# Scores of a pair's second row one set of products later in an attention-and-experts kernel on Trainium2

## The chip, the cores and the metric

The kernel runs on one core of a Trainium2 chip. The core's engines run side by side, each through its own list of instructions, and wait for each other by semaphores: TensorE (PE in the rows; PEld is its weight load), VectorE (DVE), ScalarE (ACT), GpSimd (POOL), and SyncE (SP), which here only issues DMAs. The metric is the device time of one execution in microseconds; less is better.

## The reference

Eight batch rows of 512 tokens with 256 channels are normalized, attend to 64 context tokens of their row, and go through three experts (768 to 512 to 256 channels), weighted by a softmax router, and through a gate. All is float32.

```
nx = layer_norm(x) ; q = nx @ Wq ; k = ctx @ Wk ; v = ctx @ Wv
weights  = softmax(q k^T * H**-0.5) ; evidence = weights @ v
combined = [nx, evidence, anchor]
probs  = softmax(combined @ router_W + router_b)
h      = silu(combined @ e_w1 + e_b1)           # three experts
routed = sum_e probs_e * (h_e @ e_w2 + e_b2)
g      = sigmoid(silu(combined @ gate_w1 + gate_b1) @ gate_w2 + gate_b2)
out    = x + g * (routed @ out_w + out_b)
```

## The kernel before

Two batch rows make a pair, and the loop at line 1113 runs over four pairs, j = 0 to 3. Row 2j is the pair's first row and 2j + 1 its second; in the stage of pair j, b0 and b1 are the two rows of pair j + 1, which are prepared beside it. Tokens lie along the free dimension (512), channels along the 128 partitions. A product is one matmul of a 128x128 weight with a 128x512 operand. Products of a 2x2 block form (two channel blocks by the two rows) are computed by Strassen's scheme (its Winograd form): seven products in place of eight, with sums and differences of operands formed by VectorE and GpSimd ahead.

Each pair has a gate layer (gate_layer, line 742), three expert layers (expert_layer, line 788) and the outputs stage (outputs, line 866). The order on every engine is the order of the program text; nothing reorders it. What belongs to the next pair is woven in by hand: put() in the loop hangs a step onto a named point, and run(point) emits the steps of that point in the order in which they were put.

The outputs stage runs sets of twelve products through experts(): first u (line 1006), then z with the weight sums S1 (1011), u with S2 (1016), y (1020), u (1024), z with S4 (1027) and u (1030). "S2 set", "y set" and "u set" in this text are lines 1016, 1020 and 1024. Between them VectorE forms differences of the hidden rows (subtract, line 922, whose operation is line 930), keeps partial results (keep, 944) and finishes a quarter of the output (finish, 956): sum (959), gate (960), block transpose into yb (961), then GpSimd adds x (962), and SyncE stores it in eight DMAs (951). The tag yb has two buffers.

The steps of the next pair that matter here:

- transpose_blocks(b), line 504: two VectorE block transposes (509), then two ScalarE scalings (481) that give nxT, the normalized and transposed x
- scores(b), line 523: sixteen small PE products out of nxT into one PSUM bank (531), VectorE takes the maximum (539), scales it (541, tile nmx) and copies the router's part (543, tile lg); ScalarE takes four exponentials with their sums (546)
- softmax(b), line 552: VectorE's reciprocal (555) and one multiplication of the weights w (556)
- router_logits(b), line 570: two products and two reductions over context tokens (576, 582), then four short operations
- combine_x(j + 1), line 512, on GpSimd: four differences of the two rows' nxT (521); the third overwrites a block of b1's nxT and so has to come after b1's scores
- transpose_w(j + 1), line 558, at the point P7: four PE transposes of the softmax weights of both rows, which ScalarE copies to wT

PSUM banks for small steps come from misc(), which hands out three banks in turn in the order of its calls.

Of the kernel before, what the change touches and what calls it, by code (L numbers as in the profile page):

```python
# [16 lines left out]
def kernel(  # L17
# [50 lines left out]
    nc = tc.nc  # L68
# [797 lines left out]
    def outputs(j, steps):  # L866
        last = j == NP - 1

        def run(point):
            for step in steps.get(point, ()):  # L870
                step()
# [40 lines left out]
        def a(q, i, k):  # L912
            return w2o[:, 2 * q + k, i * P : (i + 1) * P]
# [5 lines left out]
        def combo(s):  # L919
            return lambda q: w2s[:, s, q, :]  # L920

        def subtract(dst, other):

            (k, i), (k2, i2), (k3, i3) = dst, *other
            for e in range(E):
                d, p, m = (
                    S["h", ii, e].rearrange("p (q k) t -> p q k t", k=2)[:, :, kk, :]
                    for kk, ii in ((k, i), (k2, i2), (k3, i3))
                )
                nc.vector.tensor_tensor(d, p, m, ALU.subtract)  # L930
# [25 lines left out]
        def finish(r, ps, i, row):  # L956

            yb = work.tile([P, T], F32, tag="yb", name=f"yb_{2 * j + row}_{i}")
            nc.vector.tensor_tensor(r, r, ps, ALU.add)
            nc.vector.tensor_tensor(r, r, S["hg", row, i], ALU.mult)  # L960
            nc.vector.transpose(yb, r)  # L961
            nc.gpsimd.tensor_tensor(yb, yb, S["xb", 2 * j + row][:, i, :], ALU.add)  # L962
            store(yb, i, row, slice(0, T), (nc.sync,))
# [55 lines left out]
        if j + 1 < NP:  # L1019
            experts(y, lambda q: a(q, 0, 1), 1, 0, start=True)  # L1020
            finish(r11, y, 0, 0)
            subtract((0, 1), ((1, 0), (0, 1)))
            run("P2")
            experts(u, lambda q: a(q, 1, 0), 0, 0)
            finish(r22, u, 1, 1)
            run("P7")
            experts(z, combo(S4), 1, 1)
            finish(r12, z, 0, 1)
            run("P3")
            experts(u, lambda q: a(q, 1, 1), 0, 1)  # L1030
            finish(r21, u, 1, 0)
            run("P4")
            return
# [22 lines left out]
    with tc.manual_schedule(engines=None):  # L1056
        ctx_rows = context.flatten_outer_dims().rearrange("(t p) d -> p t d", p=P)
        for d in range(2):
            half = slice(d * NX // 2, (d + 1) * NX // 2)
            nc.sync.dma_start(ctx_sb[:, half, :], ctx_rows[:, half, :])  # L1060
        nc.scalar.dma_start(wk_sb, rows_of(Wk))
        nc.scalar.dma_start(wv_sb, rows_of(Wv))
        load_x(0)
        nc.sync.dma_start(wq_sb, rows_of(Wq))
        load_x(1)
        for g in (E, 0):
            load_first(g)
            load_anchor(g)
        for g in (1, 2):
            load_first(g)  # L1070

        wake(7)
        context_transposes()
        project_keys()
        statistics(0, 0, NT)
        deviation(0, 0)
        normalize(0)
        project(wv_sb, ctxT, lambda m, ps: nc.scalar.copy(vT[:, m, :], ps), "v")
        small_transposes()
        wq_transposes()  # L1080
        transpose_x(0)
        router_anchor()
        statistics(1, 0, NT)
        deviation(0, 1)
        normalize(1)
        load_table(AF.Exp)
        project(wqT, kT, keep_m, "m")
        combine_weights(E)
        value_weights(0, E)
        spread_router_rows(0)  # L1090
        transpose_x(1)
        combine_x(0, nc.vector, (0, 1))
        scores(0)
        scores(1)
        load_table(AF.Silu)
        combine_weights(0)
        softmax(0)
        value_weights(0, 0, nc.vector.tensor_copy)
        anchor_rows(E)
        anchor_rows(0)  # L1100
        softmax(1)
        combine_x(0, nc.vector, (2, 3))
        combine_weights(1)
        combine_weights(2)
        late_scratch()
        load_anchor(1)
        load_anchor(2)
        nc.sync.dma_start(ow_sb, rows_of(out_w))
        nc.sync.dma_start(gw2_sb, rows_of(gate_w2))
        combine_gate()  # L1110
        load_second(0)

        for j in range(NP):


            within, between = {}, {}

            def put(where, n, step, *args):
                where.setdefault(n, []).append(lambda: step(*args))

            if j == 0:
                put(within, "gate", value_weights, 0, 1)
                put(within, (0, "A"), anchor_rows, 1)
                put(within, (0, "A"), router_logits, 0)
                put(within, (0, "A"), load_second, 1)
                put(within, (0, "B"), second_bias)
                put(within, (0, "B"), router_logits, 1)
                put(within, (0, "C"), transpose_second, 0)
                put(within, (0, "C"), anchor_columns, 1)
                put(within, (0, "C"), anchor_rows, 2)  # L1130
                for b in range(2):
                    put(within, (0, "C"), router_exp, b)
                    put(within, (0, "D"), router, b)
                put(within, (0, "C"), load_second, 2)
                put(within, (0, "D"), second_layer, 0)
                put(within, (0, "D"), spread_probabilities, 0)
                put(within, (0, "D"), combine_second, 0)
                put(within, (1, "A"), transpose_second, 1)
                put(within, (1, "B"), second_layer, 1)
                put(within, (1, "B"), combine_second, 1)  # L1140
                put(within, (1, "C"), transpose_second, 2)
                put(within, (1, "C"), anchor_columns, 2)
                put(within, (1, "D"), second_layer, 2)
                put(within, (1, "D"), combine_second, 2)
            if j:
                put(within, "gate end", spread_probabilities, j)
            put(within, (0, "C" if j == 0 else "B"), value_weights, j, 2)
            put(within, (1, "C"), load_x_blocks, 2 * j)
            put(within, (2, "A"), gate_differences, j)
            put(within, (2, "C"), load_x_blocks, 2 * j + 1)  # L1150
            if j + 1 < NP:
                b0, b1 = 2 * j + 2, 2 * j + 3
                put(within, "gate", load_x, b0)
                put(within, "gate", load_x, b1)
                put(within, (0, "A" if j else "D"), statistics, b0, 0, NT)
                put(within, (0, "C") if j else (1, "A"), statistics, b1, 0, NT)
                for i in range(2):
                    put(within, (1, "C"), deviation, j + 1, i)
                where = (1, "D") if j else (2, "B")
                put(within, where, normalize, b0)  # L1160
                put(within, where, store_x, b0)
                put(within, where, regroup_x, b0)
                put(within, (2, "C"), normalize, b1)
                put(within, (2, "C"), store_x, b1)
                put(between, "begin", transpose_blocks, b0)
                put(between, "gate", regroup_x, b1)
                put(between, "P1", scores, b0)
                put(between, "begin", value_weights, j + 1, E)
                put(between, "begin", spread_router_rows, j + 1)
                put(between, "P5", softmax, b0)  # L1170
                put(between, "P5", transpose_blocks, b1)
                put(between, "P6", scores, b1)
                put(between, "P6", router_logits, b0)
                put(between, "P6", softmax, b1)
                put(between, "P6", combine_x, j + 1, nc.gpsimd)
                put(between, "P7", transpose_w, j + 1)
                put(between, "P7", value_weights, j + 1, 0)
                put(between, "P7", router_logits, b1)
                put(between, "P3", value_weights, j + 1, 1)
                put(between, "P3", router_exp, b0)  # L1180
                put(between, "P3", router_exp, b1)
                put(between, "P4", router, b0)
                put(between, "P4", router, b1)
            gate_layer(j, within)
            for e in range(E):
                expert_layer(j, e, within)
            outputs(j, between)
# [34 lines left out]
```

## Time and profile before

| | |
|---|---|
| median of 3 runs | 489.81 us (489.61 to 491.72) |
| profiled execution | 491.32 us, its span 489.6 us |
| mean granted TensorE clock | 0.986 |
| PE busy | 477.2 us, 97% |
| VectorE busy | 350.1 us, 72% |
| ScalarE busy | 218.0 us, 45% |
| GpSimd busy | 77.3 us, 16% |

The span runs from the first to the last instruction of the profiled execution; the rest of its time lies around it. Times in rows are microseconds from the start of the span unless ns stands beside them. A PE row's busy time runs to the modelled end of a pipelined product, so that successive rows overlap a little; in the chain of work that ended last they don't, and there the piece of a set is its share of the time. A granted clock of 1.00 is 2.4 GHz, one of 0.50 is 1.2 GHz. The three stages of pairs 0, 1 and 2 that prepare a next pair end their S2 sets at about 125, 240 and 353 us; the last pair prepares nothing.

### The profile page before, as it was taken

The page shows a single profiled execution, that of the slowest core. Times are in us where ns is not written, and L with a number is a line of the kernel's source. Part 1 is how long each engine was busy: PE and PEld are TensorE (multiplying, and loading weights), DVE is VectorE, ACT ScalarE, POOL GpSimd, SP SyncE. Part 2 cuts the span into 40 slices and gives each one's busy share as a digit, 9 for nine tenths or more (in the row PEclk, how much of TensorE's full clock was granted, in tenths as well). Part 3 has the DMA queues.
Part 4 walks back from the last instruction along what each step waited for, and adds up shares of the span by engine and source line. Part 5 has one row for each costly group of instructions (what it writes and reads, how often), then busy time and mean ns, then how long its engine had stood idle before and what let it go on. Part 6 is the DMA issues. An engine that isn't in the chain of part 4 may idle for free.

```text
span 489.6 us, 4649 instructions
## 1 busy us (share of the span) xinstructions
PE 477.2 (97%) x1451; PEld 227.8 (47%) x1451; DVE 350.1 (72%) x649; ACT 218.0 (45%) x391; POOL 77.3 (16%) x96
## 2 busy tenths in 40 slices
PE   8999999999799999999799999999899999999997
PEld 7744555445444444445444444445354444444454
DVE  2845748989786555889788555898979525787982
ACT  3455565566200556747211365758211254458000
POOL 5326024000412100000232100000042200000010
PEclk9999999999799999999989999999989999999999
DMA  9977230067012550342102550162102380000013
GB/s 283 381 114 151 39 131 0 22 132 63 17 21 43 132 151 0 81 92 43 16 3 42 132 169 2 52 119 44 18 0 43 52 207 0 1 0 1 0 18 68
DMA packets 118120, 35.27 MB, mean 72 GB/s; under 512 B 104732, under 2 KB 115088, under 8 KB 117584
## 3 DMA queue, kind: packets, MB, share of 16 engines
q1 hardware_dynamic: 114736, 27.02, 27.2%
q0 software_dynamic: 1472, 7.18, 4.6%
q10 hardware_dynamic: 1888, 0.79, 0.6%
q8 instruction: 11, 0.18, 0.2%
q14 instruction: 13, 0.11, 0.1%
HBM read 27.57 MB, written 7.40 MB: 71 GB/s over the span
## 4 chain that ended last, share of the span: by engine, by line
PE 89%; DVE 8%; ACT 1%; DMA 1%; issue 1%; DVEq 0%; ACTq 0%
PE ps_u L656 37%; PE ps_z L656 17%; PE ps_y L656 15%; PE ps_vw L631 5%; DVE h L930 4%; PE ps_s L531 3%; PE ps_gu L656 3%; PE ps_w2o L416 2%; PE ps_gz L656 1%; ACT nxT L481 1%; DMA scr_ctx<-in_ctx_dram 1%; DVE h L739 1%; PE ps_k L310 1%; PE ps_v L298 1%; PE ps_gy L656 1%
## 5 line engine op out<-in xcount | busy, mean ns | idle before, releaser
L739 DVE TENSOR_TENSOR h<-h,pb 128x512 f32<-128x512 f32 x96 | 61.9, 694 | 10.5 <-ACT h L689 10.5
L656 PE MATMUL ps_u<-h,w2o 128*128 128x512 f32 x144 | 63.8, 592 | 0.0
L656 PE MATMUL ps_u<-nxT,w 128*128 128x512 f32 x112 | 55.6, 607 | 0.0
L689 ACT ACTIVATE h<-h,abias 128x512 f32<-128x512 f32 x72 | 49.2, 718 | 8.7 <-DVE h L695 8.2
L656 PE MATMUL ps_z<-wT,vw 64*128 64x512 f32 x104 | 49.5, 605 | 0.0
L962 POOL TENSOR_TENSOR yb<-yb,xb 128x512 f32<-128x512 f32 x14 | 21.8, 1555 | 144.6 <-DVE yb L961 130.2
L656 PE MATMUL ps_z<-h,w2s 128*128 128x512 f32 x96 | 42.8, 595 | 0.2 <-DVE r L945 0.2
L656 PEld LDWEIGHTS ps_u<-h,w2o 128*128 128x128 f32 x144 | 27.3, 190 | 32.8 <-issue 30.6
L698 ACT COPY h<-ps_u 128x512 f32<-128x512 f32 x48 | 27.9, 582 | 32.2 <-PE ps_u L656 31.9
L695 DVE TENSOR_TENSOR h<-h,ps_y 128x512 f32<-128x512 f32 x24 | 16.4, 683 | 28.5 <-PE ps_y L656 28.5
L656 PEld LDWEIGHTS ps_u<-nxT,w 128*128 128x128 f32 x112 | 19.9, 189 | 29.7 <-issue 22.8
L930 DVE TENSOR_TENSOR h<-h,h 128x1024 f32<-128x1024 f32 x24 | 31.0, 1345 | 0.0
L689 ACT ACTIVATE h<-ps_u,abias 128x512 f32<-128x512 f32 x24 | 16.5, 687 | 30.4 <-PE ps_z L656 30.4
L656 PE MATMUL ps_y<-nxT,w 128*128 128x512 f32 x56 | 28.6, 592 | 0.0
L656 PE MATMUL ps_z<-T,ws 128*128 128x512 f32 x56 | 28.6, 592 | 0.0
L656 PEld LDWEIGHTS ps_z<-h,w2s 128*128 128x128 f32 x96 | 17.9, 190 | 22.1 <-issue 21.1
L656 PE MATMUL ps_u<-wT,vw 64*128 64x512 f32 x56 | 27.8, 611 | 0.0
L656 PE MATMUL ps_y<-h,w2o 128*128 128x512 f32 (+1 forms) x60 | 27.2, 612 | 0.0
L656 PE MATMUL ps_y<-wT,vw 64*128 64x512 f32 x56 | 27.0, 596 | 0.0
L631 PE MATMUL ps_vw<-w,vT 128*128 128x512 f32 (+1 forms) x64 | 26.9, 541 | 0.0
L656 PE MATMUL ps_u<-T,ws 128*128 128x512 f32 x56 | 26.7, 594 | 0.0
L656 PE MATMUL ps_z<-nxT,ws 128*128 128x512 f32 x56 | 26.6, 592 | 0.0
(206 smaller groups left out, 776.7 us busy)
## 6 DMA issues: line engine op xcount, KB each, us to landing
pb<-pd POOLq DMA_DIRECT2D x4, 1536.0 KB, 7.2
x<-in_x_dram SPq DMA_DIRECT2D x8, 512.0 KB, 5.8
xb<-in_x_dram SPq DMA_DIRECT2D x64, 64.0 KB, 2.5
out_dram<-yb SPq DMA_DIRECT2D x56, 64.0 KB, 2.0
w<-in_L_xcond_e_w_dram SPq DMA_DIRECT2D x6, 512.0 KB, 9.5
xd<-x SPq DMA_DIRECT2D x6, 512.0 KB, 3.0
xg<-xd SPq DMA_DIRECT2D x48, 64.0 KB, 2.4
scr_wa<-in_L_xcond_e_w_dram SPq DMA_DIRECT2D x3, 512.0 KB, 5.0
```

What stands on the lines that cost most here:

```text
L298: nc.tensor.matmul(ps, w_sb[:, k, m * P : (m + 1) * P], src[:, k, :], start=(k == 0), stop=(k == KH - 1))
L310: nc.tensor.matmul(ps[m][:, half], wk_sb[:, k, m * P : (m + 1) * P], ctxT[:, k, half], start=(k == 0), stop=(k == KH - 1),)
L416: nc.tensor.matmul(ps[:, d * H : (d + 1) * H], w2T[:, k, (i + d) * P : (i + d + 1) * P], ow_sb[:, k, :], start=(k == 0), stop=(k == KH - 1),)
L531: nc.tensor.matmul(ps[:, t, :], nxT[:, k, t * P : (t + 1) * P], mr[:, k, b, :], start=(k == 0), stop=(k == KH - 1),)
L631: nc.tensor.matmul(ps, vT[:, k, j * 2 * CT : (j + 1) * 2 * CT], w1[:, KH + k, n0:n1], start=(k == 0), stop=(k == KH - 1),)
L656: nc.tensor.matmul(ps, lhsT, rhs, start=start, stop=True, skip_group_check=not start)
L689: nc.scalar.activation(h, h if src is None else src, AF.Silu, bias=abias[:, c, 2 * j + i : 2 * j + i + 1])
L695: nc.vector.tensor_tensor(h, h, part, ALU.add)
L698: nc.scalar.copy(chunk(n, i, d), part)
L739: nc.vector.tensor_tensor(h, h, S["pb", j][:, i, 2 * q // RC, :], ALU.mult)
L930: nc.vector.tensor_tensor(d, p, m, ALU.subtract)
L962: nc.gpsimd.tensor_tensor(yb, yb, S["xb", 2 * j + row][:, i, :], ALU.add)
```

## The change

In the outputs stage of a pair that has a successor, the scores of b1 move from the point P6 (behind the S2 set) to the point P2 (behind the y set), with the softmax of b1 and GpSimd's combine_x. router_logits of b0 stays at P6. The point P2, which held no step, moves ahead of the subtraction that stood before it. The steps at P2 thus come behind finish(r11) and ahead of that subtraction.

```diff
         if j + 1 < NP:
             experts(y, lambda q: a(q, 0, 1), 1, 0, start=True)
             finish(r11, y, 0, 0)
+            run("P2")
             subtract((0, 1), ((1, 0), (0, 1)))
-            run("P2")
             experts(u, lambda q: a(q, 1, 0), 0, 0)
             finish(r22, u, 1, 1)
             run("P7")
...
                 put(between, "P5", softmax, b0)
                 put(between, "P5", transpose_blocks, b1)
-                put(between, "P6", scores, b1)
                 put(between, "P6", router_logits, b0)
-                put(between, "P6", softmax, b1)
-                put(between, "P6", combine_x, j + 1, nc.gpsimd)
+                put(between, "P2", scores, b1)
+                put(between, "P2", softmax, b1)
+                put(between, "P2", combine_x, j + 1, nc.gpsimd)
                 put(between, "P7", transpose_w, j + 1)
```

## Rows read from the trace of the kernel before

**Rows 1.** Page, part 1: busy us, share of the span and instructions of each engine

```profile
PE 477.2 (97%) x1451; PEld 227.8 (47%) x1451; DVE 350.1 (72%) x649; ACT 218.0 (45%) x391; POOL 77.3 (16%) x96
```

**Rows 2.** Waits of PE: line waited for, us in total, times, longest us

```profile
PE ps_s L531 <- ACT nxT L481: 7.4, 6, 2.2
```

**Rows 3.** Timeline of PE: start us, us, what, [idle before <- releaser]; stages one and two

```profile
127.69 0.44 PE L531 MATMUL ps_s<-mr,nxT 128*128 128x67 f32 x2 [2.19 <-ACT nxT L481]
...
242.19 0.44 PE L531 MATMUL ps_s<-mr,nxT 128*128 128x67 f32 x2 [2.19 <-ACT nxT L481]
```

**Rows 4.** Chain that ended last, in order of time: start us, us, what

```profile
138.72 5.15 PE ps_u L656 x12
...
227.91 1.73 PE ps_s L531 x16
...
244.67 6.90 PE ps_y L656 x12
251.57 5.15 PE ps_u L656 x12
```

**Rows 5.** Stretches of the second stage: length, engines' busy us, then PEclk, DMA

```profile
227.90:229.60 1.70, 1.70 (x18) 1.70 (x17) 1.70 (x4) 1.51 (x3) 0.00 (x0) 1.00 0.23 33
...
244.90:248.20 3.30, 3.30 (x5) 1.33 (x4) 3.23 (x5) 1.29 (x8) 2.37 (x2) 0.50 0.01 2
```

**Rows 6.** Timeline of VectorE in the second stage

```profile
240.58 1.30 DVE L509 STREAM_TRANSPOSE nxT<-xg 128x512 f32<-128x512 f32 x2
241.80 0.65 DVE L945 TENSOR_TENSOR r<-r,ps_u 128x512 f32<-128x512 f32 x1
...
245.17 0.91 DVE L541 TENSOR_SCALAR nmx<-mx 128x4 f32<-128x4 f32 x1
...
246.07 1.62 DVE L576 TENSOR_TENSOR pv<-w,vr 128x384 f32<-128x384 f32 x1
...
250.07 0.17 DVE L555 RECIPROCAL rs<-sm 128x4 f32<-128x4 f32 x1
...
251.61 0.69 DVE L959 TENSOR_TENSOR r<-r,ps_y 128x512 f32<-128x512 f32 x1 [0.91 <-PE ps_y L656]
...
253.69 4.53 DVE L930 TENSOR_TENSOR h<-h,h 128x1024 f32<-128x1024 f32 x3
```

**Rows 7.** Timeline of ScalarE in the second stage: first and last of b1's exponentials

```profile
246.24 0.31 ACT L546 ACTIVATE w<-ps_s,nmx 128x64 f32<-128x64 f32 x1 [3.40 <-DVE lg L543]
...
247.32 0.21 ACT L546 ACTIVATION_READ_ACCUMULATOR w<-ps_s,nmx 128x1 f32 x1
```

**Rows 8.** Timeline of GpSimd in the second stage

```profile
244.79 1.26 POOL L521 TENSOR_TENSOR nxT<-nxT 128x512 f32<-128x512 f32 x1
246.01 1.26 POOL L521 TENSOR_TENSOR T<-nxT,T 128x512 f32<-128x512 f32 x1
253.85 2.15 POOL L962 TENSOR_TENSOR yb<-yb,xb 128x512 f32<-128x512 f32 x1 [6.58 <-DVE yb L961]
```

**Rows 9.** Timelines of GpSimd and VectorE in the first pair's expert layers

```profile
76.06 0.72 POOL L203 TENSOR_TENSOR w2s<-w2s,w2o 128x256 f32<-128x256 f32 x1
...
83.35 1.05 POOL L203 TENSOR_TENSOR w2s<-w2s,w2o 128x256 f32<-128x256 f32 x1
...
82.01 2.95 DVE L739 TENSOR_TENSOR h<-h,pb 128x512 f32<-128x512 f32 x3
```

**Rows 10.** Timeline of PE's weight load: the first of the transposes of w

```profile
256.13 0.14 PEld L564 LDWEIGHTS pt_w<-ident,w 128*128 128x128 f32 x1 [0.24 <-issue]
```

**Rows 11.** Timeline of VectorE behind the stage's last set: its idle time

```profile
270.93 0.69 DVE L959 TENSOR_TENSOR r<-r,ps_u 128x512 f32<-128x512 f32 x1 [3.60 <-PE ps_u L656]
...
276.23 0.69 DVE L695 TENSOR_TENSOR hg<-hg,ps_u 128x512 f32<-128x512 f32 x1 [1.21 <-PE ps_u L656]
```

**Rows 12.** Stores: issue ns (min/median/max) by line; page, part 6, us to landing last

```profile
L951 SPq DMA_DIRECT2D out_dram<-yb x56: 315/496/511, 143.2 to 478.9; - x56
...
out_dram<-yb SPq DMA_DIRECT2D x56, 64.0 KB, 2.0
```

## The prediction, made before the change was run

> **What bounds the kernel now.** I read the page's engine shares first: TensorE (PE) is busy for 97% of the span [rows 1], so only its idle time and its half-speed time can be won. Then PE's list of waits: six waits of its score products for ScalarE's scaled x, 7.4 us together, are nearly all that PE idles once it is running [rows 2]. The timeline puts them in the three output stages that prepare a next pair, two per stage, 2.19 and 0.27 us, at the second row's scores (b1) [rows 2, 3]. The third stage repeats the second's rows, so the second stands for both.
>
> The DVE rows show why. The two block transposes of b1's x stand behind the subtractions, the keep of r22 and the softmax of the first row and run at 240.58; ScalarE scales after that, and PE, which ended its S2 products at 240.00, gets x at 242.19 [rows 3, 6]. Behind the wait the y set of twelve products takes 6.90 us, the next set 5.15 [rows 4]. The granted clock tells why: 0.50 (1.2 GHz) from 244.9 to 248.2, while the first row's scores, the same short products without an idle time ahead, ran at 1.00 (2.4 GHz) [rows 5]. So a stage loses the wait and the half-speed time that follows it.
>
> **What is removed.** PE's order becomes S2, y, b1's scores, u; before it was S2, b1's scores, y, u. In the second stage, from the end of S2 (240.00) to the start of the u set (251.57) now pass 11.57 us [rows 3, 4]. At full speed and without idle time it is one set, 5.15, and sixteen score products, 1.73: 6.88 [rows 4]. That saves 4.69. In the first stage S2 ends at 127.69 - 2.19 = 125.50 and the u set starts at 138.72: 13.22, so 6.34 is saved (its half-speed time was longer) [rows 3, 4]. With the third stage as the second: 6.34 + 2 x 4.69 = **15.72 us**. The new cover of x's wait is the y set: it ends at 245.15, x is complete at about 242.9, so 2.3 us are left over [rows 3, 4]. The y set itself waits for nothing that is late: its bank was released by the last expert layer, and the hidden rows it reads are weighed at the point "begin", ahead of the stage's first set's end.
>
> **What is added: a shorter way from the scores to the transposes of w.** The four PE transposes of the softmax weights (step P7) stay behind the u set. They had y and u ahead of them, now u alone. PE would reach them, in times of the second stage, at 240.00 + 5.15 + 1.73 + 5.15 = 252.03, and their first weight load comes 0.59 ahead of the end of the set (256.13 against 251.57 + 5.15), so at 251.44 [rows 4, 10]. I follow the chain on the other engines:
> - DVE: keep of r12 at 241.80 as now, done by about 242.4. Then router logits of b0, now ahead of b1's scores: 246.07 to 250.07 was 4.00, of which the first product lost 1.06 to a GpSimd sum (it ran until 247.27, DVE 0.42 longer), so 2.95 alone: to 245.35 [rows 6, 8]. That is behind the end of y, 245.15, so finish of r11 starts at 245.35, and DVE is free of its three operations 2.08 later (251.61 to 253.69), at 247.4 [rows 6].
> - GpSimd: r11's sum with x comes first now. It starts 2.24 after the start of finish (251.61 to 253.85): 247.6, and takes 1.26 as a sum of that size that meets no one, to 248.85. The four sums of combine_x, moved behind it, run back to back, 1.22 apart: from 248.85, 250.1, 251.3 and 252.6, the end at 253.8 [rows 6, 8]. The next pair needs them from its gate layer on, behind the last set, which ends near 266: no cost there.
> - DVE again: the maximum of b1's scores (out of PSUM) starts at 247.4; its scaling (nmx) comes behind it, well ahead of 248.85, and meets r11's sum. In the trace nmx took 0.91, ending as the GpSimd sum of 244.79 ended [rows 6, 8]: so 248.9. Then ScalarE's four exponentials start 0.16 after nmx and take 1.29: 249.05 to 250.35 [rows 7]. DVE waits, and everything queued behind it (softmax, the subtraction, finish of r22) waits too. Reciprocal 250.4, multiplication of w issued at 250.6 while the second of combine_x's sums runs (to 251.35), so it runs to 251.8.
> - PE has its weights at 251.85 instead of 251.44: **a wait of 0.4 per stage, 1.2 in all**. The end below is no wait (GpSimd half a us later or DVE quicker); the end above is one more sum, 1.25, if the multiplication misses the gap.
>
> That the multiplication gets in between two sums is read from the first pair's expert layers: three DVE products of two SBUF operands in 2.95 beside GpSimd sums that took 1.05 each instead of 0.72 [rows 9]: each waits for the other's instruction and then has its turn. And nmx got through at 246.08 though the next sum stood ready and began at 246.01 [rows 6, 8]. The Trainium skill, SBUF — State Buffer, section "SBUF: two separate sides", says that the port pair which VectorE and GpSimd share is an exclusive lock, held for the whole instruction by whichever starts first. It speaks against this change as far as five GpSimd sums in a row now meet the softmax, and it gives no order for what comes after an instruction; the trace's nmx agrees with the lock, [rows 9] adds the turns. With turns the sum carries 1.2; if the series kept the pair, rival 3 prices it, as an estimate from rows.
>
> **What is moved on the other queues.** ScalarE's order is the same (exponentials between the scaling of x and the copy of wT), so no table load is added. SP issues the same stores in the same order; r11's come 5 us earlier. The subtraction, 4.53 now beside r11's sum, will alternate with combine_x's last two sums and end near 257.8, as now (253.69 + 4.53 = 258.2) [rows 6]; only the last set reads it, which PE reaches near 261.3. Finish of r22 follows it, so DVE keeps its old times while PE runs 4.3 earlier. What absorbs this is DVE's idle time of 3.60 ahead of r21 and 1.21 ahead of the gate's sums [rows 11], 4.81 together: some 0.5 is left, 0.3 at the worse of the two places, and I cost it at nothing, with up to 0.3 per stage if I misplace it. r21 needs the buffer of r22's stores: eight issues of 0.50 and 2.0 to land, 6.0 [rows 12], from 261.5 to 267.5, against 268.4 when r21's block is written: covered, by 0.9.
>
> **The sum.** The profiled execution took 491.32 (span 489.6): 491.32 - 15.72 + 1.2 = **476.8**. The median, 489.81, is 1.5 below that execution. The first stage's extra half-speed time, 6.34 - 4.69 = 1.65, is about as large, and I take it that it varies between executions and goes with the change; then both lead to the same time. If the 1.5 lies elsewhere, it is 475.3; without any wait 489.81 - 15.72 = 474.1.
>
> **The rivals.**
> 1. The multiplication misses its gap and runs behind the third sum, at 252.6 + 0.4: a wait of 1.6 per stage in place of 0.4. Without a fall of the clock 476.8 + 3.6 = 480.4; with the half-speed time of the second stage behind it (6.90 - 5.15 = 1.75 each) 485.7. For it: from the issue of the multiplication (250.6) to the end of the second sum (251.35) there are only 0.75 us, and eight operations on three engines stand ahead of it. Against: most of them would move the sums along with it.
> 2. The clock falls in this stretch even without the idle time ahead. Then only 2.46 x 3 = 7.4 is won: 491.32 - 7.4 + 1.2 = 485.1. Against it stand the first row's scores at 1.00 [rows 5].
> 3. GpSimd's series keeps the pair until its end, 253.8, and the multiplication is done at 254.2: a wait of 2.8, and the half-speed time of 1.75: 4.55 a stage, 13.7 in all, 491.32 - 15.72 + 13.7 = 489.3, no change. The turns of [rows 9] speak against it.
> 4. The other side: nmx too waits for the whole series, from r11's sum through all four. Exponentials 254.1 to 255.4, multiplication done at 255.9, PE waits 4.45, with 1.75 of half speed 6.2 a stage: 491.32 - 15.72 + 18.6 = 494.2, slower by 4.4 than the median. It decides from the point where GpSimd can start its next sum ahead of a waiting DVE instruction; nmx at 246.08 speaks against it [rows 6, 8].
> 5. The change doesn't reach the wait: y is held by something that the wait now hides, and the stage keeps its length: 489.8. No row shows such a thing.
>
> **How the numbers follow.** Forecast (a wait of 0 to 0.6, 474.1 to 478): 0.64. Rival 1: 0.14; rival 2: 0.06; rival 3: 0.08; rival 4: 0.05; rival 5: 0.03. The predicted time is the forecast's, 476.8. The range runs from 474.0 to 485.7; it takes in the forecast and rivals 1 and 2, 0.84. About 0.5% (2.4 us) is what a measurement can tell from no change: faster 0.84, same (rivals 3 and 5) 0.11, slower (rival 4) 0.05.
>
> **What would show it.** Right: PE's waits for ScalarE's x are gone from the list; y takes 5.15 at a clock of 1.00; b1's scores stand at 1.73 behind it; the only new wait is that of the transposes' weights for the multiplication, some 0.4; nmx is long beside r11's sum, the multiplication long beside combine_x. Wrong: a wait of over 1 us at the transposes, a clock of 0.5 behind them, DVE late at r21 or at the gate's sums, or a y set that is not at full speed.

## The result and the profile after

The changed kernel takes 475.99 us (median of 4 runs, 475.90 to 476.25), the kernel before 490.41 beside it: ratio 0.970, 95% interval 0.968 to 0.973. The forecast was 476.8 in a range of 474.0 to 485.7. The profiled execution took 476.25, its span 474.5; the mean granted clock rose from 0.986 to 1.0, and PE is busy for 99% of the span instead of 97%.

PE's waits after (line waited for: us in total, times, longest us) answer to [rows 2]. All of them lie in the preparation or in the last pair; the wait for x, 7.4 us, has no row any more, and none took its place:

```profile
PE ps_wake L255 <- DVE warm_t L158: 1.1, 1, 1.1
PE ps_s L531 <- DVE mr L318: 0.2, 1, 0.2
PE ps_z L656 <- DVE r L945: 0.2, 1, 0.2
```

The chain that ended last, in the second stage (start us, us, what), answers to [rows 4]. From the start of the S2 set to the start of the u set pass 241.02 - 228.99 = 12.03 us, which is what the prediction summed (5.15 + 5.15 + 1.73):

```profile
228.99 5.15 PE ps_u L656 x12
234.13 5.15 PE ps_y L656 x12
239.28 1.73 PE ps_s L531 x16
241.02 5.20 PE ps_u L656 x12
246.22 0.48 PE pt_w L564 x4
```

The stretches of the same stage answer to [rows 5]: length, busy us of the engines, then PEclk and DMA. The y set and the b1 scores run at 1.00:

```profile
234.00:239.10 5.10, 5.10 (x13) 2.25 (x12) 4.93 (x12) 1.52 (x2) 0.00 (x0) 1.00 0.01 2
239.10:240.80 1.70, 1.70 (x17) 1.68 (x16) 1.60 (x5) 0.00 (x0) 0.00 (x0) 1.00 0.00 0
```

VectorE's timeline, then GpSimd's, answer to [rows 6] and [rows 8]. nmx (1.17) is long beside GpSimd's sum of 241.80, the multiplication of w (1.13) beside the one of 244.37, and the subtraction (5.63 instead of 4.53) takes turns with the last two:

```profile
239.43 0.68 DVE L959 TENSOR_TENSOR r<-r,ps_y 128x512 f32<-128x512 f32 x1
...
241.92 1.17 DVE L541 TENSOR_SCALAR nmx<-mx 128x4 f32<-128x4 f32 x1
...
244.80 1.13 DVE L556 TENSOR_TENSOR w<-w,rs 128x256 f32<-128x256 f32 x1
245.85 5.63 DVE L930 TENSOR_TENSOR h<-h,h 128x1024 f32<-128x1024 f32 x3
...
260.61 0.69 DVE L959 TENSOR_TENSOR r<-r,ps_u 128x512 f32<-128x512 f32 x1
...
265.77 0.69 DVE L695 TENSOR_TENSOR hg<-hg,ps_u 128x512 f32<-128x512 f32 x1 [0.85 <-PE ps_u L656]
```

```profile
241.80 1.26 POOL L962 TENSOR_TENSOR yb<-yb,xb 128x512 f32<-128x512 f32 x1 [12.87 <-DVE yb L961]
243.04 1.25 POOL L521 TENSOR_TENSOR T<-nxT,nxT 128x512 f32<-128x512 f32 x1
244.37 1.27 POOL L521 TENSOR_TENSOR T<-nxT,T 128x512 f32<-128x512 f32 x1
245.60 1.45 POOL L521 TENSOR_TENSOR nxT<-nxT 128x512 f32<-128x512 f32 x1
247.01 2.25 POOL L521 TENSOR_TENSOR T<-nxT,T 128x512 f32<-128x512 f32 x1
```

Last, PE's weight loads at the transposes, which answer to [rows 10]:

```profile
245.20 0.19 PEld L656 LDWEIGHTS ps_u<-h,w2o 128*128 128x128 f32 x1 [0.24 <-issue]
246.04 0.42 PEld L564 LDWEIGHTS pt_w<-ident,w 128*128 128x128 f32 x4 [0.65 <-issue]
```

```profile
240.86 5.37 PE L656 MATMUL ps_u<-h,w2o 128*128 128x512 f32 x12
246.07 0.63 PE L564 MATMUL pt_w<-ident,w 128*128 128x128 f32 x4
```

The loads of a set stand 0.43 apart. The first load for w would have come at 245.63 and came at 246.04: 0.41 late, as forecast. The transposes began 246.07 - 240.86 = 5.21 behind the start of the u set (the 5.20 of the chain), 0.05 more than the 5.15 that the prediction counted. Run 7, where the load is on time, shows the same 5.21, so these 0.05 don't come from the late load.

### The profile page after: what moved, and what is told of

Same layout as the page of the kernel before. It is cut to its first block, busy times and chain, and to the rows that moved or that the text cites. A ratio compares the mean times of both kernels' runs of the same rounds, so it can differ in the third digit from the quotient of the medians.

```text
span 474.5 us, 4652 instructions
## 1 busy us (share of the span) xinstructions
PE 469.6 (99%) x1451; PEld 225.1 (47%) x1451; DVE 353.4 (74%) x649; ACT 218.4 (46%) x391; POOL 78.2 (16%) x96
## 4 chain that ended last, share of the span: by engine, by line
PE 94%; DVE 4%; issue 1%; ACT 0%; ACTq 0%
PE ps_u L656 42%; PE ps_z L656 18%; PE ps_y L656 15%; PE ps_vw L631 5%; PE ps_gu L656 3%; PE ps_s L531 3%; PE ps_w2o L416 2%; PE ps_gz L656 1%; DVE h L930 1%; PE ps_wake L255 1%; PE ps_k L310 1%; DVE h L739 1%; PE ps_gy L656 1%; PE ps_v L298 1%; PE ps_ar L354 0%
## 5 line engine op out<-in xcount | busy, mean ns | idle before, releaser
L962 POOL TENSOR_TENSOR yb<-yb,xb 128x512 f32<-128x512 f32 x14 | 19.1, 1365 | 149.5 <-DVE yb L961 145.2
L930 DVE TENSOR_TENSOR h<-h,h 128x1024 f32<-128x1024 f32 x24 | 34.3, 1483 | 0.0
L656 PE MATMUL ps_u<-T,w 128*128 128x512 f32 x56 | 26.6, 592 | 0.0
```

The lines of the kernel that those rows point to most:

```text
L656: nc.tensor.matmul(ps, lhsT, rhs, start=start, stop=True, skip_group_check=not start)
```

## The experiments

The theory: the change removes PE's idle time ahead of b1's scores and the half-speed time behind it, and the shortened way to the transposes of w is still covered. The rivals that had to be told apart from it were a clock that falls in this stretch anyway, and a lock between GpSimd and VectorE that costs PE time. Each kernel ran beside the kernel before on the same chip (medians of before 490.97 to 491.01). "Run" and a number mean the experiment of that number below.

One thing to know for the sizes: a product call of 128x512 is two rows of 0.43 us in the trace, so that a set of twelve rows is six calls. Where the text above counts twelve products in a set, or sixteen score products, these are rows: six calls and eight.

**1. PE works through the wait, too long.** The kernel before, with five calls ahead of b1's scores into the bank that the scores then overwrite:

```diff
-        ps = misc(f"ps_s_{b}")[:, : NT * SC].rearrange("p (t c) -> p t c", c=SC)
+        ps = misc(f"ps_s_{b}")
+        if j and i:
+            for _ in range(5):
+                nc.tensor.matmul(ps, ident, w1[:, 0, :512], start=True, stop=True)
+        ps = ps[:, : NT * SC].rearrange("p (t c) -> p t c", c=SC)
```

> The kernel before, with five products that nobody reads (128x512, 0.43 us each) put ahead of the second row's scores, so that PE works through the 2.19 us in which it waits for x. Order and waits stay as before. Theory (the half-speed time behind the wait comes from PE's idle time): y runs in 5.15 at a clock of 1.00, and a stage takes 2.15 + 0.27 + 1.73 + 5.15 = 9.3 from the end of S2 to the u set instead of 11.57 (second, third) and 13.22 (first): 8.4 us less than before, 491.3 - 8.4 = 483 us. Rival 2 (the clock falls in this stretch without idle time too): the rows of before stay, 490 us. If the idle time itself were all that the change removed, this kernel would gain nothing.

Measured 488.79 (488.25 to 489.28). The filling was mis-sized: five calls are ten rows, 4.29 us, twice the wait, so the scores came some 2 us later than x allowed. The clock was 0.999 and the y set ran at full speed, so the half-speed time did go, but the excess gave most of it back. A smaller filling was needed for the size.

**2. The filling cut to the wait.**

```diff
+            for n in (512, 512, 256):
+                nc.tensor.matmul(ps[:, :n], ident, w1[:, 0, :n], start=True, stop=True)
```

> As e1_fill, with the filling cut to what the wait can hold: e1's five calls were ten product rows of 0.43 us, 4.29 in all, and pushed the scores back by 2.1. Here two calls of 512 columns and one of 256: 2.15 us. PE works through the wait, order and length stay as before. Theory (the half-speed time comes from the idle time): 2.15 + 0.3 + 1.73 + 5.15 = 9.3 from the end of S2 to the u set instead of 11.57 and 13.22: 491.0 - 8.4 = 482.6 us. Rival 2: 490 to 491.

Measured 484.61 (484.51 to 485.07): 6.4 less than before, with every wait and all of before's order in place. PE's timeline of the second stage, and the clock of it (PEclk third from the end):

```profile
236.57 2.31 PE L531 MATMUL ps_s<-w,ident 128*128 128x512 f32 x6
238.92 0.44 PE L535 MATMUL ps_s<-mr,nxT 128*128 128x67 f32 x2
239.63 1.78 PE L535 MATMUL ps_s<-mr,nxT 128*128 128x67 f32 x14 [0.27 <-ACT nxT L481]
241.24 5.37 PE L660 MATMUL ps_y<-h,w2o 128*128 128x512 f32 x12
246.44 5.31 PE L660 MATMUL ps_u<-h,w2o 128*128 128x512 f32 x12
```

```profile
238.90:246.40 7.50, 7.21 (x28) 4.25 (x29) 5.07 (x10) 1.97 (x9) 4.97 (x4) 1.00 0.00 1
```

The scores still start when x comes, 2.35 behind the start of the filling, but nothing behind them is slow. So the half-speed time is the consequence of PE's idle time; rival 2 is out. The expectation was 2 us too low: from the end of S2 to the u set pass 246.44 - 236.57 = 9.87, not 9.3 (the filling ends before x comes, the 0.27 stays, and the set behind the scores takes 5.20). This run splits the gain: **6.4 us are the clock, the other 8.6 (484.61 to 475.99) what the waits cost at full speed.** PE's list shows 7.4 of these 8.6 as idle time [rows 2].

**3. A shorter idle time.** As 2, with one call of 0.86 us, so that 1.33 of the idle time stays.

```diff
+            nc.tensor.matmul(ps, ident, w1[:, 0, :512], start=True, stop=True)
```

> As e5_fill_2us with one call only, 0.86 us: 1.33 of the idle time stays. No work is taken away or added on the way that ends last, so the time depends on the clock alone: 482.6 if an idle time of 1.33 leaves it at 1.00, 490 to 491 if it falls as behind 2.19. The run e4_one_first, where 0.7 left it at 1.00, speaks for the first.

Neither of the two times: 489.73, in ten executions between 487.74 and 491.65 that lie in three groups by their mean clock, about 488.0 (0.993), 489.8 (0.989 to 0.990) and 491.4 (0.984 to 0.986). The profiled one (488.2) shows all three stages to wait alike, and the clock to fall behind two of the waits only (from 242 to 244 and from 354 to 356 it stands at 0.50; the stretches below are longer):

```profile
128.00:136.00 8.00, 7.73 (x30) 4.48 (x31) 5.50 (x13) 1.92 (x9) 4.98 (x4) 1.00 0.00 0
...
239.10:243.00 3.90, 3.62 (x18) 2.96 (x19) 1.03 (x3) 0.67 (x1) 3.69 (x3) 0.72 0.00 0
...
352.00:356.00 4.00, 3.73 (x18) 3.08 (x19) 0.96 (x3) 0.58 (x1) 3.67 (x3) 0.68 0.00 0
```

An idle time of 1.33 followed by one of 0.27 may bring the half speed or not, from stage to stage and from execution to execution. The kernel before has such groups too: of the 19 executions beside this run, six lie at 489.5 to 490.2 with a clock of 0.990 and thirteen at 490.6 to 491.8 with 0.984 to 0.986.

**4. The subtraction ahead of the scores again**, one part of the change undone:

```diff
-            run("P2")
             subtract((0, 1), ((1, 0), (0, 1)))
+            run("P2")
```

> The changed kernel with one part undone: the subtraction stands ahead of the scores' VectorE part again. Theory: VectorE reaches the maximum of b1's scores only when the subtraction is done, some 4.8 us later than in the changed kernel (its three operations with one turn of a GpSimd sum), the multiplication of w is done at about 249 to 249.5 instead of 245.9 (second stage, times of the changed kernel), and PE waits 3 us ahead of the transposes in each stage, with the clock at 0.50 behind it: 3 x (3 + 1.75) = 14 on 476.0, 490 us. If the clock stays at 1.00 behind such a wait: 485. If the place of the subtraction does not matter: 476.

Measured 497.54 (496.86 to 499.21), slower than before: ratio 1.0146, 1.0119 to 1.0174. PE's wait moves to the transposes:

```profile
PE pt_w L564 <- DVE w L556: 14.6, 3, 4.9
```

The mechanism is the expected one, its size not: 4.9 us a stage instead of 3. The subtraction takes turns with GpSimd's sums (5.60 us), nmx waits for the third of them and the multiplication for the last, and between these two VectorE waits 1.42 for the four exponentials. Behind the wait the clock is 0.50:

```profile
258.40:263.00 4.60, 4.59 (x9) 2.54 (x10) 1.87 (x3) 0.64 (x2) 1.26 (x1) 0.50 0.09 16
```

At the median, 497.54 - 475.99 = 21.6, of which 14.6 is waiting; the other 7.0 is half speed, 2.3 a stage. So the place at which P2 runs is worth more than the whole gain of the change: without it, moving the scores loses.

**5 and 6. One and two of the three subtraction operations ahead of the softmax**, which make w late by chosen amounts (the diff is that of one; the other has range(2)):

```diff
             run("P2")
-            subtract((0, 1), ((1, 0), (0, 1)))
+            subtract((0, 1), ((1, 0), (0, 1)), range(1))
+            run("P2b")
+            subtract((0, 1), ((1, 0), (0, 1)), range(1, E))
...
-                put(between, "P2", softmax, b1)
-                put(between, "P2", combine_x, j + 1, nc.gpsimd)
+                put(between, "P2b", softmax, b1)
+                put(between, "P2b", combine_x, j + 1, nc.gpsimd)
```

> The changed kernel with the first of the subtraction's three operations put between the scores' VectorE part and the softmax, which makes w late by a chosen amount: it waits for a GpSimd sum, runs 1.2, and the multiplication waits for the next sum: done about 1.3 later. Theory: PE waits 1.2 per stage ahead of the transposes, 476.0 + 3.6 = 479.6 if the clock stays at 1.00 behind an idle time of 1.2; 485 if it falls as behind 2.19 (rival 1's two prices). If the time stays at 476.0, the transposes had more room than the rows say.

> As e4_one_first with two of the subtraction's three operations ahead of the softmax. Each costs one operation and one turn of a GpSimd sum, 2.3 to 2.5 us, of which the wait for the exponentials hides about 1.4 once: PE waits about 3.2 at the transposes (0.7 in e4_one_first, 4.9 in e2_sub_first). Theory: the clock falls behind 3.2, as behind 4.9, where it cost 2.3 a stage: 476.0 + 3 x (3.2 + 2.3) = 492.5. If it holds: 485.6.

One operation: 478.13 (478.02 to 478.44), 2.1 above the changed kernel. PE waits 0.7 a stage, 2.1 in all, and the clock stays at 1.0: the time is the wait and no more. Less than the 1.2 expected: in the second stage w is done 0.86 later than in the changed kernel (measured from the start of the u set), not 1.3. Two operations: 488.50, in ten executions between 487.62 and 491.54; PE waits 2.9 a stage, 8.6 in all. Their waits to the transposes:

```profile
PE pt_w L564 <- DVE w L556: 2.1, 3, 0.7
```

```profile
PE pt_w L564 <- DVE w L556: 8.6, 3, 2.9
```

475.99 + 8.6 = 484.6, so 3.9 of the median, 1.3 a stage, is half speed; the time lies between the two that were expected (485.6 and 492.5); the executions again lie in groups by clock (0.993: 487.6 to 488.6; 0.990: 489.6 and 489.9; 0.986: 491.5).

**7 and 8. GpSimd's sums away from the softmax**, then once more beside the changed kernel (run 8 and a repeat of the changed kernel):

```diff
-                put(between, "P2", combine_x, j + 1, nc.gpsimd)
+                put(between, "P7", combine_x, j + 1, nc.gpsimd)
                 put(between, "P7", transpose_w, j + 1)
```

> The changed kernel with GpSimd's four sums (combine_x) put behind finish of r22, so that they no longer run beside b1's softmax. Theory (the lock delays VectorE, but its delay is covered on PE): the multiplication takes 0.42 instead of 1.13 and the subtraction 3.5 instead of 5.6, PE's wait at the transposes goes from 0.05 to 0, and the time stays at 476.0 within 0.3. If the sums beside the softmax cost PE what the prediction put there (0.4 per stage): 474.8. If the sums come too late for the next gate layer, whose second product reads the first of them: a wait of PE for GpSimd there and over 478.

> The changed kernel as it is, beside e10_sums_late_again on the same chip: 476.0 us as measured before. Its profile had 0.05 of a wait per stage ahead of the transposes of w, so that at most 0.2 us is to be had from the order of GpSimd's sums.

> e3_sums_late once more (combine_x behind finish of r22), beside the changed kernel on one chip, to see whether its 475.8 is less than the changed kernel's 476.0. Theory: PE's way is shorter by 0.05 a stage, 0.15 in all, which the comparison can hardly resolve: 475.8 to 476.0. If the lock between GpSimd and VectorE cost more than PE's rows show: 475 or less.

Measured 475.79 (475.54 to 476.10) in the first comparison; in the second 476.27 (475.58 to 478.36) against 475.83 (475.64 to 476.03) for the changed kernel, whose ratio to before was again 0.970 (0.968 to 0.972). So the two are the same. One of the five executions of run 8 took 478.36, 2.1 us above the other four, at a clock of 1.0; no trace shows why. VectorE's rows show that combine_x's sums no longer hold up the softmax: the multiplication is back at 0.42, the subtraction at 3.49; nmx still meets r11's sum.

```profile
241.23 1.17 DVE L541 TENSOR_SCALAR nmx<-mx 128x4 f32<-128x4 f32 x1
...
244.10 0.42 DVE L556 TENSOR_TENSOR w<-w,rs 128x256 f32<-128x256 f32 x1
244.44 3.49 DVE L930 TENSOR_TENSOR h<-h,h 128x1024 f32<-128x1024 f32 x3
```

With the multiplication done at 244.52, the first load for the transposes is on time, 0.43 ahead of them. Yet they begin 245.37 - 240.16 = 5.21 behind the start of the u set, just as in the changed kernel, where it is 0.41 late; only the four of them take 0.60 instead of 0.63:

```profile
240.16 5.37 PE L656 MATMUL ps_u<-h,w2o 128*128 128x512 f32 x12
245.37 0.60 PE L564 MATMUL pt_w<-ident,w 128*128 128x128 f32 x4
```

```profile
244.94 0.14 PEld L564 LDWEIGHTS pt_w<-ident,w 128*128 128x128 f32 x1 [0.24 <-issue]
```

So combine_x's sums cost VectorE some 2.9 us a stage in the changed kernel (0.71 in the multiplication, 2.14 in the subtraction) and PE 0.03.

**9. Another cure.** The kernel before, its order of scores kept, with b1's block transposes between the stage's first two subtractions (lines 1012 and 1013):

```diff
         subtract((0, 1), ((1, 1), (0, 1)))
+        run("P1b")
         subtract((0, 0), ((0, 1), (0, 0)))
...
-                put(between, "P5", transpose_blocks, b1)
+                put(between, "P1b", transpose_blocks, b1)
```

> Another cure on the kernel before: the old order of the scores, but the two block transposes of b1's x stand between the two subtractions, some 4.5 us earlier on VectorE, so that x is complete near 238.6 when S2 ends at 240.0 (second stage of before). Theory (what counted was PE's wait for x and the clock behind it, not the order of y and the scores): both go here too, 6.34 + 2 x 4.69 = 15.7 less, 475.6 us. If the order of y itself brought something: more than 476.5. If the second subtraction, now 1.3 later, is late for its set: a wait of PE for it and over 478.

Measured 476.97 (476.26 to 477.09), ratio 0.972 (0.969 to 0.974). With x complete ahead of the end of S2, the second and third stages have no wait and a clock of 1.00. In the first stage 0.34 and 0.45 are left, because VectorE itself waited 2.61 for the regrouped x from memory. PE's rows of the first and of the second stage:

```profile
125.83 0.44 PE L531 MATMUL ps_s<-mr,nxT 128*128 128x67 f32 x2 [0.34 <-ACT nxT L481]
126.72 1.78 PE L531 MATMUL ps_s<-mr,nxT 128*128 128x67 f32 x14 [0.45 <-ACT nxT L481]
...
234.81 1.90 PE L531 MATMUL ps_s<-mr,nxT 128*128 128x67 f32 x16
236.55 5.37 PE L656 MATMUL ps_y<-h,w2o 128*128 128x512 f32 x12
```

The time is above the 476.5 from which the expectation would have given the order of y a worth of its own, but the stages say otherwise: from the start of the S2 set to the first product behind the transposes of w, this run takes 17.68 in the second stage and the changed kernel 17.71. The first stage alone is longer, by 1.28 (18.95 against 17.67). So the order of y and the scores is worth nothing by itself: what counts is that PE never stands idle for x.

## Why the prediction was right

**What bounds it, and what is removed.** The removed term was 15.72 us. In the timelines of PE the three stages go from 18.37, 16.72 and 16.72 (start of S2 to start of u) to 12.03, 12.04 and 12.04: that is what was taken out. Runs 1 and 2 show that the half speed belonged to the idle time, run 9 that the wait for x was its only cause.

**Execution and median.** The prediction held that the first stage's longer half-speed time varies between executions and goes with the change. Before, 42 executions, over all comparisons, lie between 488.0 and 491.8, in groups by clock; after, nine lie between 475.6 and 476.3 at a clock of 0.998 to 1.0. So the variation goes with the change. That it is the first stage that varies is not shown: there is one trace of the kernel before. The sum against the profiled execution (491.32) was the right one, as that execution belongs to the larger group; the alternative of 475.3 by the median would have been 0.7 too low.

**The way to the transposes.** In the second stage S2 ends 5.87 us earlier after than before. With that taken off, the chain was forecast to start the finish of r11 at 239.48 and started it at 239.43; GpSimd's sum 241.73 and 241.80; nmx's end 243.03 and 243.09; the multiplication issued 244.73 and 244.80, done 245.93 and 245.93. The multiplication did get in between two sums, and rivals 1, 3 and 4 did not come about. The series of sums was not left alone behind it: the subtraction took its turns, and GpSimd's last sum ended 1.3 later than the 247.93 that the chain put down (249.26). The prediction said that they would alternate but did not carry it into that end; nobody waited for it.

**The first miss: the step from the late load to PE's wait.** The prediction put a wait of 0.4 per stage, 1.2 in all, because the weights came 0.41 later than their load would have been issued. The load was 0.41 late, but the transposes began no later for it: 5.21 behind the start of the u set, with the late load and without it (run 7). A weight load that runs ahead of the last product of a set stands 0.43 ahead of its own product, and here 0.41 of these 0.43 were free. What the late load cost is 0.03 in the four transposes, and in the first stage, where it was 0.32 late, nothing. Run 5 shows that the room is then used up: in its second stage w is done 0.86 later than in the changed kernel (246.88 against 245.93, the stage itself 0.09 later), and the transposes begin 0.87 later behind the start of the u set (6.08 against 5.21).

The sum missed a smaller term of another kind: a set right behind the short score products takes 5.20 and not 5.15, for y as for u (runs 2, 7 and 9). Both terms together are some 0.2 in all three stages, where the prediction put 1.2. With them its sum gives 491.32 - 15.72 + 0.2 = 475.8, below the profiled execution of 476.25. That execution came to its first S2 set 0.42 later than the one before the change (120.61 against 120.19), in a part in which the two kernels are the same. So the wait was put 1.0 too high, this difference of 0.4 between executions hid part of it, and that the forecast came within 0.55 of the profiled execution is partly luck.

**The remainder on the other queues.** VectorE's idle time ahead of r21, 3.60 [rows 11], was used up entirely, and 0.85 of the 1.21 ahead of the gate's sums is left, where the prediction expected some 0.5 of the two together. No PE wait came of it. The stores, ScalarE's order and the buffer of yb cost nothing that the rows show.

**The rivals' prices.** Rival 1's wait of 1.6 was not tried as such. Beside it stand 0.7 without any loss of clock (run 5), 1.33 with a loss in some stages (run 3), 2.9 with 1.3 a stage at the median (run 6) and 4.9 with 2.3 (run 4). The 1.75 that the prediction took from the second stage of before lies among them, as a size that varies. Rival 4's outcome, a softmax so late that the change loses, can be had, but by another mechanism: in run 4 the subtraction, and not the series of sums, makes it late.

## What to carry to other kernels

Where TensorE is busy nearly throughout, look for its few idle times and price each one together with the slow stretch behind it: here waits that cost 8.6 us brought another 6.4 at half speed. Put work that depends on nothing late in front of work that waits, but follow the moved step's own successors on every engine, since the wait can move there (run 4 ended 6.5 us above the kernel before, with the changed kernel's order on TensorE). And before crediting a late weight load to TensorE, see how much of the load's lead was free.

## What the runs showed of the hardware that was not expected

- The granted clock fell behind short idle times, and not always. Behind 0.7 us it stayed at 1.00 (2.4 GHz) in all three stages (run 5); behind 1.33, with 0.27 after it, it fell to 0.50 (1.2 GHz) in part of the stages and executions (run 3); behind 2.19, with the same 0.27, it fell in all three stages of the profiled execution before. The same kernel so has groups of executions about 1.7 us apart, and its spread is less once the idle time is gone (before 3.8 us over 42 executions, after 0.6 over nine).
- A scaling of 128x4 elements takes 0.17 us alone (kernel before) and 1.17 when a GpSimd sum of two operands has just begun, while maxima out of PSUM (0.39 to 0.42) and reciprocals (0.18) beside such sums keep their time. With long operations on both sides the two engines take turns: three subtraction operations of 1.2 us took 5.63 beside two sums. The Trainium skill, SBUF — State Buffer, section "SBUF: two separate sides", calls the shared port pair an exclusive lock, held for the whole instruction; nmx at 1.17 agrees. Who comes next it leaves open, and here it was the one that had waited.
- A weight load 0.41 us late, of a lead of 0.43, did not delay the start of its product (5.21 behind the start of the set either way); the four transposes took 0.03 longer.
- A set of twelve rows takes 5.15 us behind another set and 5.20 right behind the sixteen rows of score products, all at a clock of 1.00.
